# A graph layer on one core: rows of every 68th quad fetched by SyncE, another order on VectorE, another start

## The chip, the core and the metric

The kernel runs on one core of a Trainium2 chip. The metric is the device time of one execution in microseconds, the median of several. The engines are named as in the profile: PE (TensorE, matmuls; PEld is its weight load), DVE (VectorE), ACT (ScalarE), POOL (GpSimd) and SP (SyncE, which only issues DMAs here). [...]

## What is computed

One message-passing layer on a graph of 12,500 nodes and 400,000 edges, the edges sorted by destination. Each node has 160 features: 64 scalars and 32 vectors of three. Everything is float32.

```python
h_s = s @ lin1_ws * a * _inv(S_IN)                      # per node, and h_v likewise
hid = jax.nn.silu(edge_scalars @ fc_w1 * _inv(R))       # per edge
w = hid @ fc_w2 * _inv(FC_HID)                          # 224 weights per edge
es = h_s[edge_src]; ev = h_v[edge_src]                  # rows of the source nodes
m_s1 = w1 * es * e0                                     # messages, five kinds
...
agg_s = jax.ops.segment_sum(mid_s, edge_dst, num_segments=n) * inv_nn
o_s = agg_s @ lin2_ws * a * _inv(S_MID)                 # per node, and o_v likewise
...
x = _layernorm(x + gated)
```

The host only lays inputs out (transposes, tiles of 128 edges, each edge on one of the 128 partitions).

## The kernel before

**The start.** Node features come transposed in six chunks of 2048 nodes and one of 212 (`CH`, `starts`): `xa` (scalars and two of the three vector components) in two halves of columns, and `xz` (the third component) in four quarters on four groups of 32 partitions. PE multiplies them with the block-diagonal weights `l1` and `l1z` (L316, L331), DVE scales the result with the node attribute into `ht` (L319, L334), and a DMA on ACT's queue stores `ht` to the table `h_tab` in DRAM (L345). SP's queue holds, in this order: `rows`, the first destination of each block of three tiles (three strided loads of single elements, L254, L255); the features; the first indices `idx`, edge attributes `eat` and edge scalars `es`; the weights of the edge MLP, `w1` and `w2`, in twelve loads. `dt`, all destinations, is loaded on ACT's queue after the stores (L351). From it DVE makes `rel`, the place of each edge's destination relative to its block's base (L387). All engines' instructions of the start stand in the order in which they are written (`manual_schedule`).

**The loop.** 3125 tiles of 128 edges are taken in 782 steps of up to four tiles, a *quad*: two tiles of each half of a chunk of 24 tiles. A step `n` does, in this order:

- `fetch(n + 4)`: loads of a chunk's `es` (two DMAs of 384 KB) and of the next 72 tiles' `idx` and `eat` when a quad four steps ahead is the first to need them.
- `gather` (L427): four indirect DMAs on POOL, each fetching the 128 rows of one tile from `h_tab` (640 bytes each) into `hg`, in a pool of four buffers (`deep`). POOL does nothing else in the loop.
- `weights` (L440): PE multiplies the hidden layer `hid` with `w2` into `pw` (two buffers in PSUM).
- `products` (L450, L458): DVE multiplies `pw` with `hg` into `pr`, four instructions.
- `select_quad`: DVE compares `rel` with a ramp into a one-hot matrix `oh` (L504) and multiplies it with the edge attributes into `sel` (L507).
- up to two additions of finished blocks to the sums `acc` (L546), which read their place from registers.
- `sum_up` for the quad of two steps before (L514): PE multiplies `sel` with `pr` into `pa`, the segment sum of a block; ACT copies a finished pair of blocks to `sa` (L706).
- `hide(n + 2)` (L418, L420): the hidden layer of a later pair of quads, on PE and ACT.
- turning blocks over (`pt` L523, copies `tt` L526, L528), and for 16 blocks at a time the second linear map (`po` L538, copy `os` L541), for whose bases DVE loads registers from `rows` (L730).
- some steps also carry the self connection and the end of finished nodes (transposes, gates, layer norm, store).

On PE, DVE, ACT and POOL the order of the loop is the written one; on SP the framework orders the loads. A DMA of SP or ACT takes one of eight semaphores in turn, and waits until the DMA that had it before has landed.

A path for edges whose destinations lie too far apart follows the loop; with these inputs it isn't entered.

Of the kernel before, what the change touches and what calls it, by code (L numbers as in the profile page):

```python
# [10 lines left out]
F32 = mybir.dt.float32  # L11
I32 = mybir.dt.int32
I16 = mybir.dt.int16
BF16 = mybir.dt.bfloat16
AF = mybir.ActivationFunctionType
OP = mybir.AluOpType
AX = mybir.AxisListType
# [17 lines left out]
CT = 2 * SIDE  # L35
AHEAD = 3 * CT
NF = 4

MARGIN = 128
NO = 16  # L40
# [13 lines left out]
def gnn_kernel(  # L54
# [40 lines left out]
    in_order = ctx.enter_context(ExitStack())  # L95
    in_order.enter_context(tc.manual_schedule(
        engines={ENG.PE, ENG.DVE, ENG.Activation, ENG.Pool, ENG.SP}))
    at = consts.tile([P, NT], F32, name="at")
    nc.scalar.dma_start(at, attr)

    l1 = consts.tile([P, P], F32, name="l1")
    nc.vector.memset(l1, 0.0)
    nc.scalar.dma_start(l1[:S, :S], lin1_ws)
    for i in range(2):
        r = slice(S + i * V, S + (i + 1) * V)
        nc.scalar.dma_start(l1[r, r], lin1_wv)
    scales = [(l1[:S], 1.0 / math.sqrt(S)), (l1[S:], 1.0 / math.sqrt(V))]

    def scale():
        for m, by in scales:  # L110
            nc.vector.tensor_scalar_mul(m, m, by)
        scales.clear()

    def block_diagonal(name, w, n, scale, queue=nc.scalar):
        k = w.shape[0]
        m = consts.tile([n * k, n * k], F32, name=name)
        nc.vector.memset(m, 0.0)
        for i in range(n):
            queue.dma_start(m[i * k:(i + 1) * k, i * k:(i + 1) * k], w)
        if scale != 1.0:  # L120
            scales.append((m, scale))
        return m

    l1z = block_diagonal("l1z", lin1_wv, 4, 1.0 / math.sqrt(V))
    for m, by in scales:
        nc.scalar.mul(m, m, by)
    scales.clear()


    rel = consts.tile([P, TT], I16, name="rel")  # L130
    rows = consts.tile([1, NB], I32, name="rows")
    early = consts.tile([1, 1], F32, name="early")
# [84 lines left out]

    ess = {}

    def load_chunk(c):  # L220
        if c in ess:
            return
        t0, halves = chunks[c]
        es = ess[c] = loads.tile([2 * S, SIDE * P], F32, name="es")
        for half, n in enumerate(halves):
            to = es[half * S:(half + 1) * S]
            e0 = (t0 + half * halves[0]) * P
            nc.sync.dma_start(to[:, :n * P], es_t[:, e0:e0 + n * P])


    ident = consts.tile([P, P], F32, name="ident")
# [16 lines left out]
                   base=0, channel_multiplier=0)  # L248
    nc.gpsimd.iota(share[:, even:], pattern=[[RATE, NB - even]], base=even * RATE, channel_multiplier=0)

    with nc.allow_non_contiguous_dma(reason="the first destination of each block"):
        firsts = dst[0:1, 0:(even - 1) * BT + 1:BT].rearrange("o (c h k) -> o h c k", k=KB, h=2)
        for half in range(2):
            nc.sync.dma_start(in_pairs(rows[:, :even])[:, half], firsts[:, half])  # L254
        nc.sync.dma_start(rows[:, even:], dst[0:1, even * BT:(NB - 1) * BT + 1:BT])  # L255


    U = 4
    dt = ends_pool.tile([P, TT], I32, name="dt")
    lo = ends_pool.tile([P, NB], F32, name="lo")  # L260
# [2 lines left out]
    with tc.tile_pool(name="nodes", bufs=len(starts)) as nodes, tc.tile_pool(  # L263
        name="nodes_ps", bufs=6, space=PSUM
    ) as nps, tc.tile_pool(name="z_ps", bufs=2, space=PSUM) as zps:
        loaded = []
        for c0 in starts:
            cn = min(CH, N - c0)
            quarters = 4 if cn == CH else 1
            assert quarters == 4 or cn <= U * P  # L270
            xa = nodes.tile([P, CH], F32, name="xa")
            for b0 in range(0, cn, CH // 2):
                b1 = min(b0 + CH // 2, cn)
                nc.sync.dma_start(xa[:S, b0:b1], xs_t[:, c0 + b0:c0 + b1])
                nc.sync.dma_start(xa[S:, b0:b1], xv_t[:2 * V, c0 + b0:c0 + b1])
            xz = nodes.tile([P, U * P], F32, name="xz")
            cq = cn // quarters
            for q in range(quarters):
                nc.sync.dma_start(xz[q * V:(q + 1) * V, :cq],
                                  xv_t[2 * V:, c0 + q * cq:c0 + (q + 1) * cq])  # L280
            loaded.append((c0, cn, quarters, cq, xa, xz))
        index(0)
        load_chunk(0)
        for half in range(2):
            r = slice(half * S, (half + 1) * S)
            nc.sync.dma_start(w1[r, r], fc_w1)
            at_c = 0
            for a, b in ((64, 128), (0, 64), (192, 224), (160, 192), (128, 160)):
                nc.sync.dma_start(w2[r, half, at_c:at_c + b - a], fc_w2[:, a:b])
                at_c += b - a  # L290

        def bases():

            base_f = ends_pool.tile([1, NB], F32, name="base_f")
            nc.vector.tensor_copy(base_f, rows)
            for b0 in range(0, NB, U * P):
                b1 = min(NB, b0 + U * P)
                ps = nps.tile([P, U, P], F32, name="hp").rearrange("p u c -> p (u c)")
                nc.tensor.matmul(ps[:, :b1 - b0], ones, base_f[:, b0:b1], start=True, stop=True)
                nc.scalar.copy(lo[:, b0:b1], ps[:, :b1 - b0])  # L300
            nc.vector.tensor_sub(share, rows, share)
            nc.vector.tensor_reduce(early, share, AX.X, OP.min)
            nc.vector.tensor_scalar(early, early, -float(MARGIN), None, op0=OP.is_lt)

        for c0, cn, quarters, cq, xa, xz in loaded:
# [19 lines left out]
                                            at[:n, first + full:first + full + 1], None, op0=OP.mult)  # L325

            pz = zps.tile([P, U, 4, V], F32, name="pz")
            k = quarters * V
            for u in range(-(-cq // P)):
                n = min(P, cq - u * P)  # L330
                nc.tensor.matmul(pz[:n, u, :quarters].rearrange("p q c -> p (q c)"),  # L331
                                 xz[:k, u * P:u * P + n], l1z[:k, :k], start=True, stop=True)
            if quarters == 4:
                nc.vector.tensor_mul(  # L334
                    ht[:, :, P:].rearrange("p (q u) c -> p u q c", q=4), pz,
# [5 lines left out]
            if cn > full * P:  # L341
                n = cn - full * P
                nc.vector.tensor_scalar(ht[:n, full, P:], pz[:n, full, 0],
                                        at[:n, first + full:first + full + 1], None, op0=OP.mult)
            nc.scalar.dma_start(  # L345
                h_tab[c0:c0 + full * P, :].rearrange("(q p) d -> p q d", p=P), ht[:, :full])
            if cn > full * P:
                nc.scalar.dma_start(h_tab[c0 + full * P:c0 + cn, :], ht[:n, full])


    nc.scalar.dma_start(dt, dst)  # L351
    iota = consts.tile([P, W], F32, name="iota")
    nc.vector.tensor_copy(iota, iota_i)
    nc.vector.tensor_scalar_mul(w2, w2, 1.0 / math.sqrt(64))

    scs = consts.tile([S, V3], F32, name="scs")
    nc.sync.dma_start(scs, sc_ws)
# [65 lines left out]
    def gather(pool, idx):  # L423
# [5 lines left out]
                in_offset=bass.IndirectOffsetOnAxis(ap=i, axis=0))  # L429
        return hg  # L430

    def weights(psum, hid, slots):

        pw = psum.tile([P, Q, 256], F32, name="pw")
        n = len(slots)
        for t in range(0, n, 2):
            half, c = slots[t]
            m = min(2, n - t)
            assert half == 0 and all(slots[t + k] == (k, c) for k in range(m))
            nc.tensor.matmul(pw[:, t:t + m, :NWT], hid[:m * S, c * P:(c + 1) * P], w2[:m * S, :m],  # L440
                             start=True, stop=True)
        return pw
# [52 lines left out]
            sorted_eat[a0] = eas  # L495
        return sorted_eat[a0]

    def select_quad(pool, tiles):

        n = len(tiles)  # L500
        t0 = slot_of[tiles[0][0]]
        u = t0 % AHEAD
        oh = pool.tile([P, Q, W], F32, name="oh4")[:, :n]
        nc.vector.tensor_tensor(oh, rel[:, t0:t0 + n, None].to_broadcast([P, n, W]),  # L504
                                iota[:, None, :].to_broadcast([P, n, W]), op=OP.is_equal)
        sel = pool.tile([P, Q, 4, W], F32, name="sel", bufs=3)
        nc.vector.tensor_mul(  # L507
            sel[:, :n], oh[:, :, None, :].to_broadcast([P, n, 4, W]),
            by_slot(tiles[0][0])[:, u:u + n, :, None].to_broadcast([P, n, 4, W]))
        return sel  # L510
# [112 lines left out]
    with tc.tile_pool(  # L623
        name="fin", bufs=1
    ) as fin, tc.tile_pool(
        name="late", bufs=2
    ) as late, tc.tile_pool(name="edge", bufs=2) as edge, tc.tile_pool(
        name="deep", bufs=4
# [26 lines left out]
        def fetch(n):  # L655

            if n < len(steps):
# [2 lines left out]
                    load_chunk(c)  # L660
                for t, _, _ in tiles:
                    ahead(t)

        def hide(n):

# [109 lines left out]
                    turning.extend(job[:nt])  # L775
                    doing.extend(job[nt:])

        with tc.manual_schedule(engines={ENG.PE, ENG.DVE, ENG.Activation, ENG.Pool}):
            fetch(0)
            hide(0)  # L780
            waits = []
            pieces = list(range(0, N, CHN))
            products_due = []
            checks = farthest(late)
            for n, (c, i, tiles) in enumerate(steps):
                if 2 <= n < 2 + ZP // 2:
                    for k in range(2):
# [1 line left out]
                if n in checks:  # L789
                    checks[n]()  # L790
                fetch(n + 4)
                hg = gather(deep, [index(t) for t, _, _ in tiles])
                pw = weights(pw_ps, hids[c, i // 2], [(half, u - i // 2 * 4) for _, half, u in tiles])

                rest = turning.pop(0)() if turning else None
# [3 lines left out]
                def first(n=n):  # L799
                    if rest:  # L800
                        rest()
                    ready.extend(add_up(n))

                pr = products(edge, pw, hg, len(tiles), [first, lambda n=n: ready.extend(add_up(n))])
                sel = select_quad(edge, tiles)
                for a in ready:
                    add(*a)
                if step_on:
                    step_on()
                begin()  # L810
# [153 lines left out]
```

## Time and profile before

| | |
|---|---|
| median of 15 runs | 5032.44 us (5026.09 to 5071.89) |
| the profiled execution | 5034.64 us, span 5032.8 us |
| granted TensorE clock, mean | 0.883 |
| PE, DVE, POOL, ACT busy | 79%, 48%, 60%, 18% of the span |
| gathers (L427) | 3125, 967 ns mean, first at 78 us |
| first products (L450) | 92 us |
| DMA, 20 to 80 us | 95% busy, 259 GB/s |
| DMA, 100 to 4990 us | 31% busy, 80 GB/s |

Times are from the start of the span. A line of the waits has: the engine and line that waited, what ended the wait, us in total, times, longest. "issue" means that the engine waited for nothing that the profile shows, "remote" that a semaphore's update could not be put down to an instruction. A line of the timeline has: start, length, engine, line, operation, output and inputs, how many instructions are merged, and in brackets the engine's idle time before and what ended it. [...]

### The profile page before, as it was taken

To read this page: it belongs to the slowest core of one execution; us is meant where nothing else is said; L and a number is where in the kernel's file an instruction comes from. 1 tells how busy PE (TensorE), PEld (TensorE's weight loads), DVE (VectorE), ACT (ScalarE), POOL (GpSimd) and SP (SyncE) were. 2 spreads that over 40 slices of the span, in tenths; PEclk is the share of its full clock that TensorE was granted. 3 is DMA by queue.
4 is the path that set the end of the run, shared out by engine and by line. 5 is a ranking of instruction groups with operands and counts; after the bars stand their busy time and mean duration, and the time that the engine had idled before them with its cause. 6 is when DMAs were issued, how large, how long until landed. Compare 5 with 4: busy or idle time off the path is not lost. (4 is left out here: it accounts for less than half of the span.)

```text
span 5032.8 us, 47627 instructions
## 1 busy us (share of the span) xinstructions
PE 3978.8 (79%) x14291; PEld 1698.3 (34%) x14291; DVE 2433.0 (48%) x6374; ACT 926.7 (18%) x2463; POOL 3026.4 (60%) x3134
## 2 busy tenths in 40 slices
PE   5788787887778877887777877878878787878877
PEld 3333333333333333333333333333333333333333
DVE  4544444544544544544544544444544544544544
ACT  1211111211211111212111111111121211211212
POOL 3666665666666666665665665666666666666663
PEclk7898898988988888989898888989988898889888
DMA  7233332332333333333333233323333332333221
GB/s 196 76 81 77 78 83 74 83 85 75 81 80 81 81 81 78 83 79 79 81 81 80 75 85 77 77 78 86 78 82 80 80 86 75 81 81 80 76 72 51
DMA packets 241211, 411.77 MB, mean 82 GB/s; under 512 B 74200, under 2 KB 171876, under 8 KB 240820
## 3 DMA queue, kind: packets, MB, share of 16 engines
q0 software_dynamic: 150000, 256.20, 19.5%
q1 hardware_dynamic: 77666, 142.75, 11.7%
q10 hardware_dynamic: 13282, 9.69, 0.7%
q8 instruction: 119, 1.95, 0.2%
q14 instruction: 144, 1.18, 0.1%
HBM read 392.40 MB, written 16.00 MB: 81 GB/s over the span
## 5 line engine op out<-in xcount | busy, mean ns | idle before, releaser
L427 POOL DMA_INDIRECT hg<-h_tab,idx x3125 | 3021.7, 967 | 1962.5 <-DVE oh L504 984.3
L440 PE MATMUL pw<-w,hid 128*128 128x448 f32 x3126 | 1519.0, 613 | 294.9 <-ACT hid L420 98.5
L450 DVE TENSOR_TENSOR pr<-pw,hg 128x512 f32<-128x512 f32 x782 | 539.4, 690 | 2332.5 <-remote 1093.3
L514 PE MATMUL pa<-pr,sel 128*64 128x416 f32 x6250 | 1384.7, 557 | 101.1 <-issue 65.7
L458 DVE TENSOR_TENSOR pr<-pw,hg 128x384 f32<-128x384 f32 x2346 | 1154.3, 547 | 2.3 <-issue 2.2
L440 PEld LDWEIGHTS pw<-w,hid 128*128 128x128 f32 x3126 | 608.1, 213 | 837.3 <-issue 659.1
L514 PEld LDWEIGHTS pa<-pr,sel 128*64 128x64 f32 x6250 | 406.8, 144 | 1011.8 <-issue 869.5
L523 PE MATMUL pt<-ident,sa 128*128 128x128 f32 x2084 | 357.9, 297 | 296.8 <-ACT hid L420 162.5
L706 ACT COPY sa<-pa 128x416 f32<-128x416 f32 x521 | 265.9, 510 | 1751.3 <-remote 657.9
L418 PE MATMUL ph<-es,w 128*128 128x512 f32 (+1 forms) x784 | 453.2, 661 | 71.0 <-ACT tt L528 38.1
L523 PEld LDWEIGHTS pt<-ident,sa 128*128 128x128 f32 x2084 | 255.4, 149 | 634.9 <-issue 339.2
L420 ACT ACTIVATE hid<-ph 128x512 f32<-128x512 f32 x392 | 234.5, 598 | 1079.2 <-remote 612.6
L538 PE MATMUL po<-tt,l 128*96 128x256 f32 (+5 forms) x1496 | 369.4, 397 | 43.8 <-ACT tt L528 30.5
L507 DVE TENSOR_TENSOR sel<-oh,eas 128x256 f32<-128x256 f32 x782 | 338.5, 433 | 42.7
L526 ACT COPY tt<-pt 128x192 f32<-128x192 f32 x521 | 166.2, 319 | 770.9 <-remote 231.5
L538 PEld LDWEIGHTS po<-tt,l 128*96 128x96 f32 (+1 forms) x1496 | 239.4, 172 | 191.9 <-issue 84.9
L418 PEld LDWEIGHTS ph<-es,w 128*128 128x128 f32 x784 | 120.0, 193 | 340.2 <-issue 255.0
L546 DVE TENSOR_TENSOR acc<-acc,os 96x32 f32 x1042 | 195.0, 187 | 26.1 <-ACT os L541 6.9
L504 DVE TENSOR_TENSOR oh<-rel,iota 128x64 f32<-128x64 int16 x782 | 170.1, 217 | 0.5 <-issue 0.5
L572 PE MATMUL pp<-ident,acc 96*128 96x96 f32 x196 | 38.6, 285 | 107.7 <-DVE acc L546 48.8
L528 ACT COPY tt<-pt 128x64 f32<-128x64 f32 x521 | 117.0, 225 | 0.0
L541 ACT COPY os<-po 96x512 f32<-96x512 f32 (+2 forms) x68 | 38.3, 564 | 394.0 <-PE po L538 83.5
(77 smaller groups left out, 648.9 us busy)
## 6 DMA issues: line engine op xcount, KB each, us to landing
es<-in_es_t_dram SPq DMA_DIRECT2D x260, 384.0 KB
hg<-h_tab,idx POOLq DMA_INDIRECT x3125
h_tab<-ht ACTq DMA_DIRECT2D x6, 1280.0 KB
xt<-in_x_dram SPq DMA_DIRECT2D x23, 320.0 KB
out_dram<-y SPq DMA_DIRECT2D x23, 320.0 KB
xv<-in_xv_t_dram SPq DMA_DIRECT2D x25, 187.5 KB
xs<-in_xs_t_dram SPq DMA_DIRECT2D x25, 125.0 KB
xa<-in_xs_t_dram SPq DMA_DIRECT2D x12, 256.0 KB
```

What stands on the lines that cost most here:

```text
L418: nc.tensor.matmul(ph[:k, c], w1[:k, :k], es[:k, t0 * P + c0 * P:t0 * P + c1 * P], start=True, stop=True)
L420: nc.scalar.activation(hid[:k, c], ph[:k, c], AF.Silu, scale=1.0 / math.sqrt(64))
L427: nc.gpsimd.indirect_dma_start(out=hg[:, t, :], out_offset=None, in_=h_tab, in_offset=bass.IndirectOffsetOnAxis(ap=i, axis=0))
L440: nc.tensor.matmul(pw[:, t:t + m, :NWT], hid[:m * S, c * P:(c + 1) * P], w2[:m * S, :m], start=True, stop=True)
L450: nc.vector.tensor_mul(two, pw[:, :n, :2 * S].rearrange("p t (k c) -> p t k c", k=2), hg[:, :n, None, :S].to_broadcast([P, n, 2, S]))
L458: nc.vector.tensor_mul(pr[:, :n, first:first + V3].rearrange("p t (i c) -> p t i c", i=3), pw[:, :n, None, 2 * S + k * V:2 * S + (k + 1) * ...
L507: nc.vector.tensor_mul(sel[:, :n], oh[:, :, None, :].to_broadcast([P, n, 4, W]), by_slot(tiles[0][0])[:, u:u + n, :, None].to_broadcast([P ...
L514: nc.tensor.matmul(pa[half * ROWS:(half + 1) * ROWS, :NPR], sel[:, t].rearrange("p k w -> p (k w)"), pr, start=start, stop=stop)
L523: nc.tensor.transpose(pt[:, four * P:four * P + k], sa[:k, c:c + P], ident[:k, :k])
L538: nc.tensor.matmul(po[:, k, :nb], l2[r, terms[to, part, four]], a[:, :nb], start=(n == 0), stop=(n == len(of) - 1))
L546: nc.vector.tensor_add(window, window, os[:, :, b])
L706: nc.scalar.copy(sa, pas.pop(j)[:, :NPR])
```

## The change

It has three parts.

1. **Rows by SP.** The quads 76, 144, ..., 756 (eleven) no longer gather on POOL. Eight steps before the first of these fetches SP loads the four tiles' indices as rows of one partition each (`places`), DVE multiplies them by the 640 bytes of a row, and SP, 66 steps before the quad, begins to fetch its 512 rows one by one into `hq` (one buffer): every second step it loads 16 indices into registers and issues 16 DMAs of one row, with the address from the register. The loop's order on SP is now the written one too.
2. **DVE's order.** A step does its products, then `sel`, then the additions, then the one-hot matrix of the next step. The additions are two in even steps and one in odd ones.
3. **The start.** The first chunk's features are the first loads on SP; the loads of a chunk are one for each of `xs_t` and `xv_t` and one for `xz` (whose 128 partitions now hold the quarters interleaved, as `l1z` does). The strided loads of `rows` are gone: row 0 of `dt` is loaded on ACT's queue and DVE picks `rows` from it. `w2` is loaded as a whole (`raw`) and scaled into place by ten DVE instructions. The stores of `h` (but the last, of 84 rows, which goes to SP), the first chunk's `es` and `dt` are issued by POOL, in front of the gathers.

```diff
+OWN = 68
+BATCH = 16
+EVERY = 2
...
-    with nc.allow_non_contiguous_dma(reason="the first destination of each block"):
-        firsts = dst[0:1, 0:(even - 1) * BT + 1:BT].rearrange("o (c h k) -> o h c k", k=KB, h=2)
-        for half in range(2):
-            nc.sync.dma_start(in_pairs(rows[:, :even])[:, half], firsts[:, half])
-        nc.sync.dma_start(rows[:, even:], dst[0:1, even * BT:(NB - 1) * BT + 1:BT])
...
-            for b0 in range(0, cn, CH // 2):
-                b1 = min(b0 + CH // 2, cn)
-                nc.sync.dma_start(xa[:S, b0:b1], xs_t[:, c0 + b0:c0 + b1])
-                nc.sync.dma_start(xa[S:, b0:b1], xv_t[:2 * V, c0 + b0:c0 + b1])
+            nc.sync.dma_start(xa[:S, :cn], xs_t[:, c0:c0 + cn])
+            nc.sync.dma_start(xa[S:, :cn], xv_t[:2 * V, c0:c0 + cn])
...
+        load(starts[0])
+        at = consts.tile([P, NT], F32, name="at")
+        nc.scalar.dma_start(at, attr)
...
+        nc.scalar.dma_start(dt[0:1], dst[0:1])
+        for c0 in starts[1:]:
+            load(c0)
         index(0)
-        load_chunk(0)
+        raw = ends_pool.tile([2 * S, NWT], F32, name="raw")
         for half in range(2):
             r = slice(half * S, (half + 1) * S)
             nc.sync.dma_start(w1[r, r], fc_w1)
-            at_c = 0
-            for a, b in ((64, 128), (0, 64), (192, 224), (160, 192), (128, 160)):
-                nc.sync.dma_start(w2[r, half, at_c:at_c + b - a], fc_w2[:, a:b])
-                at_c += b - a
+            nc.sync.dma_start(raw[r], fc_w2)
...
-            nc.scalar.dma_start(
+            nc.gpsimd.dma_start(
                 h_tab[c0:c0 + full * P, :].rearrange("(q p) d -> p q d", p=P), ht[:, :full])
             if cn > full * P:
-                nc.scalar.dma_start(h_tab[c0 + full * P:c0 + cn, :], ht[:n, full])
-
-
-    nc.scalar.dma_start(dt, dst)
+                nc.sync.dma_start(h_tab[c0 + full * P:c0 + cn, :], ht[:n, full])
+
+
+    load_chunk(0, nc.gpsimd)
+    nc.gpsimd.dma_start(dt, dst)
...
+    def places(pool, n):
+        at_bytes = pool.tile([Q, P], I32, name="at_bytes")
+        for k, (t, _, _) in enumerate(steps[n][2]):
+            g, u = divmod(t, GT)
+            with nc.allow_non_contiguous_dma(reason="the indices of one tile"):
+                nc.sync.dma_start(at_bytes[k:k + 1], src[g][:, u:u + 1].rearrange("p u -> u p"))
+        return at_bytes
+
+    def rows_of(pool, at_bytes):
+        hq = pool.tile([P, Q, D], F32, name="hq", bufs=1)
+        flat_hq = hq.rearrange("p t d -> p (t d)").bitcast(U8)
+
+        def job(t, p0):
+            _, values = nc.values_load_multi_w_load_instructions(
+                at_bytes[t:t + 1, p0:p0 + BATCH], engines=[ENG.SP], min_val=0,
+                max_val=(N - 1) * row_bytes,
+                skip_runtime_bounds_check_because="every entry of src is the index of a node")
+            for p, v in enumerate(values, p0):
+                nc.sync.dma_start(flat_hq[p:p + 1, t * row_bytes:(t + 1) * row_bytes],
+                                  by_bytes[ds(v, row_bytes)][None])
+
+        return hq, [lambda t=t, p0=p0: job(t, p0) for t in range(Q) for p0 in range(0, P, BATCH)]
...
+        def fetch_rows(n):
+            for m in own:
+                if n == max(1, m - OWN - 6):
+                    at_of[m] = places(mine, m)
+                if n == m - OWN + 2:
+                    nc.vector.tensor_scalar_mul(at_of[m], at_of[m], float(row_bytes))
+                    hq_of[m], jobs = rows_of(mine, at_of[m])
+                    rows_due.extend((m, job) for job in jobs)
+            if n % EVERY == 0 and rows_due:
+                rows_due.pop(0)[1]()
...
-        with tc.manual_schedule(engines={ENG.PE, ENG.DVE, ENG.Activation, ENG.Pool}):
+        with tc.manual_schedule(engines={ENG.PE, ENG.DVE, ENG.Activation, ENG.Pool, ENG.SP}):
...
-                hg = gather(deep, [index(t) for t, _, _ in tiles])
+                fetch_rows(n)
+                hg = hq_of.pop(n) if n in own else gather(deep, [index(t) for t, _, _ in tiles])
...
-                    ready.extend(add_up(n))
-
-                pr = products(edge, pw, hg, len(tiles), [first, lambda n=n: ready.extend(add_up(n))])
-                sel = select_quad(edge, tiles)
+                    for _ in range(2 - n % 2):
+                        ready.extend(add_up(n))
+
+                pr = products(edge, pw, hg, len(tiles), [first, lambda: None])
+                sel = select_quad(edge, tiles, oh)
                 for a in ready:
                     add(*a)
+                if n + 1 < len(steps):
+                    oh = one_hot(edge, steps[n + 1][2])
```

## The prediction, made before the changed kernel ran

> **What bounds the kernel now.** I read the page's busy shares first, then the waits, then the timeline of a stretch in the middle, then that of the start.
>
> ```profile
> PE 3978.8 (79%) x14291; PEld 1698.3 (34%) x14291; DVE 2433.0 (48%) x6374; ACT 926.7 (18%) x2463; POOL 3026.4 (60%) x3134
> ```
> ```profile
> DVE pr L450 <- remote: 1093.3, 127, 14.3
> POOL hg L427 <- DVE oh L504: 984.3, 241, 10.7
> POOL hg L427 <- issue: 932.6, 2797, 72.8
> ...
> DVE pr L450 <- DMA hg<-h_tab,idx: 123.9, 63, 6.9
> ```
>
> No engine is full by the shares. But POOL's 60% leaves out 0.30 us of "issue" after every gather: in the timeline gathers follow each other every 1.25 us, so a quad's four take 5.0 us. From the first (78 us) to the last (4989 us) POOL does only two things: 3022 + 860 us of gathering (the 72.8 us before the first gather taken off), and 984 us in 241 pauses (4.1 us each) in which all four `hg` buffers are full. A quad takes 4911 / 782 = 6.28 us. DVE waits directly for a gather in only 124 us; its long waits (remote, PE) are for PE's signal. The timeline shows what these are:
>
> ```profile
> 1023.62 5.25 PE L538 MATMUL po<-tt,l 128*96 128x256 f32 x22
> ...
> 1031.36 0.95 POOL L427 DMA_INDIRECT hg<-h_tab,idx  x1 [0.30 <-issue]
> ...
> 1034.55 0.58 ACT L541 COPY os<-po 96x512 f32<-96x512 f32 x1 [10.13 <-PE pw L440]
> 1034.61 0.69 DVE L450 TENSOR_TENSOR pr<-pw,hg 128x512 f32<-128x512 f32 x1 [11.05 <-PE pw L440]
> ...
> 1036.97 0.95 POOL L427 DMA_INDIRECT hg<-h_tab,idx  x1 [4.66 <-DVE oh L504]
> ```
>
> PE's last `po` matmul ends at 1028.87, yet ACT may read `po` only at 1034.55 and DVE the next `pw` at 1034.61: 5.7 us with the work done and its signal not there. POOL's last gather had ended at 1032.31. The same happens at 1013.84 (last gather ended at 1012.51). Then DVE takes its 2.2 us of products, a buffer is free, POOL goes on. So PE and DVE stand still, POOL fills what buffers there are, and the signal comes about when POOL is quiet. Counting POOL's unbroken runs of gathers in its timeline: 102 of 248 are of exactly 16, the four quads that `deep` has buffers for; they hold 408 of the 782 quads, 52%.
>
> **Rows of every 68th quad by SP.** Quads 76, 144, ... 756, eleven, lose their gathers: 44 x 1.25 = 55 us of POOL's work. What it is worth lies between two ends. If the loop goes at POOL's cycle (16 gathers, a pause), an own quad rides along free: 6.28 us x 11 = 69 us. If PE sets the pace, nothing. I take 52% of the 69, the share of quads in full 16-gather runs: **-36 us**. Below nothing it could go by the next paragraph.
>
> SP pays: 11 x 512 row DMAs and 352 loads of 16 register values. SP's DMAs take 0.348 us (idx, median) to 0.582 us (es); DVE's register load of block bases (L730) 1.1 us. A job of 16 rows is so 16 x 0.348 + 1.1 = 6.7 to 16 x 0.582 + 1.1 = 10.4 us, and has two steps, 12.6 us. SP mostly waits today. Each row DMA also waits for the eighth DMA before it, which binds only from 8 x 0.35 = 2.8 us of landing time on. The loop's loads are now in SP's hand-written order behind jobs and output stores: the `es` of a chunk is asked for four steps and needed two steps before its first quad, a cover of 12.6 us; an index column is needed when a buffer frees, and then POOL loses what SP is late. I cost this at nothing while a job fits. The waits added: SP's first load of a batch waits for DVE's scaling of the indices (eleven small DVE operations, nearest row 0.20 us for 32x96, 2 us in all, in DVE's idle half) and for `hq` to be free; behind it stand `es` loads, asked for with that cover; DVE's products of an own quad wait for 512 rows whose last job is issued four steps before.
>
> The row says POOL's issue time is the scarce thing and DMA engines are not (31% busy from 100 to 4990 us). [...]
>
> **DVE's order.** `oh` moves behind `sel` and the additions of the step before: 0.22 us x 782 is neither added nor removed; it now falls into DVE's wait for `pw`, where there is one. Nobody waits for `sel` at once, since a quad's `pa` matmuls come two steps later: PE's `pa` waits that DVE's oh and sel end are 32.5 us (37 times) and 22.0 us (25 times). At most 62 x 0.22 = 14 us; I take **-5**. POOL's release hangs on the products, which stay first. The additions (2 or 1 a step instead of up to 2) keep their total.
>
> **The start.**
>
> ```profile
> 7.22 0.53 SPq L274 DMA_DIRECT2D xa<-in_xs_t_dram  x1
> ...
> 34.01 3.75 PE L316 MATMUL hp<-l,xa 128*128 128x128 f32 x16 [8.22 <-DMA xa<-in_xv_t_dram]
> ...
> 78.13 1.13 POOL L427 DMA_INDIRECT hg<-h_tab,idx  x1 [72.77 <-issue]
> ...
> 85.49 6.24 DVE L387 TENSOR_TENSOR rel<-dt,lo 128x260 int16<-128x260 int32 x12
> ...
> 92.13 0.67 DVE L450 TENSOR_TENSOR pr<-pw,hg 128x512 f32<-128x512 f32 x1
> ```
>
> The first features are issued at 7.2 us, behind strided one-row loads; from 20 to 80 us DMA is 95% busy at 259 GB/s, PE waiting for features. So the start is transfer-bound: features first saves 7.2 - 0.8 = 6.4 us. Fewer, larger loads and one load instead of five for the MLP weights change no bytes. DVE's extra copies (three rows, nearest row 0.68 us for 1x1042; ten scalings for one of 0.39) lie in its waits of 8 to 14 us. The stores of `h` move from ACT (0.37 us each to issue) to POOL, in front of the first `es`, of `dt` and of all gathers. No row shows a plain store from POOL. A gather of 128 rows takes it 0.95 us; a store names 2048 rows of the same 640 bytes. If cost goes by instruction, six stores are 7.5 us; if by rows, 15.2 us each. A chunk's load and store are 2.6 MB, 10.1 us at 259 GB/s, so up to that the stores hide. Beyond it the first gather comes at about 13 + 6 x 15.2 = 104 plus 2 to 3 us instead of 78: +28. I take the hidden case, **-6** (from -8 to +28); `dt` lands later relative to the stores but, with them, earlier than 85.5, and `rel` (6.2 us) follows it as now.
>
> [...]
>
> **Sum.** The profiled execution took 5034.64 us (span 5032.8); the median of 15 runs, 5032.44, is 2.2 lower. 5034.6 - 36 - 5 - 6 - 2.2 = **4985 us**.
>
> **Rivals.**
> - A, the rows are hidden anyway: PE (3979 us busy, 79%, at a granted clock of 0.883) sets the pace and POOL only pauses longer, its 984 us growing by 55. For it: only 124 us of direct waits for gathers. Against it: 52% of quads in full-buffer runs. 5034.6 - 11 - 2.2 = 5021.
> - B, SP becomes the bound: 68 steps are 427 us; less some 17 us for `es`, `idx`, `eat` and stores, a job may take 12.8 us (0.73 us a row). Each microsecond beyond costs 11 x 32 = 352 us: 13.5 us gives 5034.6 + 246 - 13 = 5268, slower. For it: no row shows a DMA with a register address. Against: both ends of the job lie below.
> - C, the quiet moments go: if PE's signals also wait for SP's rows, which are under way in over half of the time, every pause grows; 0.2 us more in each of 241 eats the gain, 1 us gives 5034.6 + 241 - 47 - 2 = 5226. Against: from 8 to 66 us SP issues loads every 0.5 to 2 us with DMA 95% busy, and DVE follows PE within 0.2 to 1.0 us there.
> - D, POOL's stores cost by rows: 4985 + 34 = 5019.
>
> **Numbers.** Forecast 0.52, A 0.20, B 0.08, C 0.12, D 0.08. 0.3% (15 us) is what a measurement of this kernel can tell from no change. The forecast's own range goes from 5032.4 - 69 - 14 - 8 = 4941 to A's side; with A and D, 0.80 lie between 4940 and 5060 (the +28 with nothing else gained). Faster: most of the forecast and a little of A, 0.53; same: A, D and the forecast's edge, 0.26; slower: B, C and the worst of D, 0.21.
>
> **What would show it.** Right: gathers down to 3081, POOL's busy down by some 43 us and its pauses hardly longer; row DMAs on SP at 0.35 to 0.6 us, a job well under 12.6 us; DVE's products of own quads without a wait for `hq`; first gather near 72 us, first product near 86. Wrong: pauses longer by what the gathers lost (A), SP solid between batches and POOL waiting for `idx` or PE for `es` (B), longer waits on remote (C), h stores of 15 us on POOL (D).

## The result, and the profile after

The changed kernel takes **5195.58 us** (median of 12 runs) against 5040.5 us (62 runs): ratio **1.0306**, 95% interval 1.0286 to 1.0326. It is slower by 155 us, where 47 us of gain were predicted; the range (4940 to 5060 us) doesn't hold it. The profiled execution has a span of 5212.0 us at a granted clock of 0.868.

One thing must be known to read what follows. The sets of runs fell on several chips and times. In three of them the kernel before takes 4081 to 4091 us, and in the traces PE's signals come at once (0.03 us after its matmuls on average in after_again); in the others, those of the prediction among them, it takes 5032 to 5130 us (medians) and PE's signals come late (2.0 us on average in before). I call these *prompt* and *late* signals, and compare times only within a set; where ratios or traces of two sets stand side by side, the text says so or names both runs.

The page's line of busy time:

```profile
PE 3966.2 (76%) x14291; PEld 1713.0 (33%) x14291; DVE 2351.3 (45%) x6397; ACT 922.3 (18%) x2463; POOL 2972.1 (57%) x3100
```

POOL has lost its 44 gathers, and every engine's share has fallen: all wait more. For what, the waits tell (us in total, times, longest):

```profile
DVE pr L494 <- remote: 1356.2, 163, 17.6
POOL hg L442 <- DVE pr L502: 1188.1, 278, 11.0
POOL hg L442 <- issue: 885.2, 2765, 6.9
...
POOL hg L442 <- DMA hq<-h_tab: 25.1, 7, 8.9
PE ph L433 <- DMA es<-in_es_t_dram: 19.5, 3, 16.0
POOL hg L442 <- DMA idx<-in_src_dram: 15.2, 3, 6.4
```

POOL's pauses on full buffers (ended by DVE's `oh` in the trace of before, by its products in that of after, as DVE's order changed) grew from 241 of 4.08 us to 278 of 4.27 us, +204 us. From its first to its last gather POOL took 4911 us before and 5102 after. The 191 us between are these 204, less 64 of gathering, and 51 of more issue time and of smaller waits. The waits for something that SP fetched late (the last three lines) are 60 us, 16 of them a single wait for the first `es`, which start_2, without rows, has too (14.0 us). So the loop isn't simply waiting for SP's loads.

A late signal like the one shown of before, in the timeline of after:

```profile
595.82 25.91 SPq L471 DMA_DIRECT2D hq<-h_tab  x32
...
599.37 1.62 PE L563 MATMUL pa<-pr,sel 128*64 128x416 f32 x8
...
601.88 1.67 PE L484 MATMUL pw<-w,hid 128*128 128x448 f32 x4
...
605.02 0.66 PE L572 MATMUL pt<-ident,sa 128*128 128x128 f32 x4
...
612.47 0.95 POOL L442 DMA_INDIRECT hg<-h_tab,idx  x1 [0.30 <-issue]
615.39 0.51 ACT L772 COPY sa<-pa 128x416 f32<-128x416 f32 x1 [16.58 <-remote]
...
616.14 0.69 DVE L494 TENSOR_TENSOR pr<-pw,hg 128x512 f32<-128x512 f32 x1 [10.61 <-remote]
...
618.49 0.95 POOL L442 DMA_INDIRECT hg<-h_tab,idx  x1 [5.07 <-DVE pr L502]
```

PE's last matmul ends at 605.7; the last of the twelve `pa` matmuls whose sum ACT copies has ended at 601.0, and the `pw` that DVE's products wait for at 603.5. Yet PE, DVE and ACT stand still until 615.4, two microseconds after POOL's last gather ended (613.4). All this time SP works through two jobs of rows that take 25.9 us.

From the semaphore events of the trace one can take, for each PE instruction that signals, the time from its modelled end to PE's next event: 2.0 us on average before, 2.7 us after (100 to 5000 us). Within after it is 3.0 us where the matmul ends during a job of rows (1777 signals) and 1.8 us where it ends between jobs (660). These averages are too high, and more so after: the traces lack some events (2236 of PE's are there for 2597 signals before, 2165 for 2592 after), and where one is missing the next is taken for it. The instructions that wait give a measure without events, the time from PE's modelled end, or from the waiting engine's own last work if that is later, to their start. ACT's copies of `pa` are late by 1.71 us before and 1.77 after (0.09 in after_again, a run with prompt signals below). DVE's products, less what they wait for gathers, are late by 1.90 and 2.12 us, but by 2.14 in no_rows_3 too, a run below without rows. So the lateness is there; that the rows make the average signal later can't be told from this.

SP's rows, in the answer for their lines (min/median/max ns, first and last start), after:

```profile
L471 SPq MOVE hq<-h_tab x5632: 2/29/1412, 142.5 to 5007.0; - x195
L471 SPq DMA_DIRECT2D hq<-h_tab x5632: 2/227/1398, 142.6 to 5007.8; - x195
```
```profile
L466 SPq TENSOR_LOAD <-at_bytes x352: 3/1216/1896, 141.3 to 4992.8; - x176
```

The medians make a job of 16 x 0.256 + 1.2 = 5.3 us. But the longest instructions, and the starts, tell another thing: from the first to the last DMA of a job it takes 9.4 us (median), as SP itself is held up every few rows. Its waits in the queue's view sum to 4087 us before and 685 us after: SP went from mostly idle to 87% taken.

The start did better than predicted:

```profile
0.75 0.59 SPq L239 DMA_DIRECT2D xa<-in_xs_t_dram  x1
...
62.20 1.04 POOL L442 DMA_INDIRECT hg<-h_tab,idx  x1 [6.92 <-issue]
...
69.46 6.34 DVE L402 TENSOR_TENSOR rel<-dt,lo 128x260 int16<-128x260 int32 x12 [12.61 <-ACT eas L530]
...
80.67 0.68 DVE L494 TENSOR_TENSOR pr<-pw,hg 128x512 f32<-128x512 f32 x1
```

The first gather is 15.9 us earlier, the first product 11.5 us. POOL's stores of `h` (L354) took 1.15 us each in the median and 1.39 at most, not 15.

### The profile page after: what moved, and what is told of

The parts are those of the page before. It is cut to its first block, busy times and chain, and to the rows that moved or that the text cites. A ratio compares the mean times of both kernels' runs of the same rounds, so it can differ in the third digit from the quotient of the medians.

```text
span 5212.0 us, 59292 instructions
## 1 busy us (share of the span) xinstructions
PE 3966.2 (76%) x14291; PEld 1713.0 (33%) x14291; DVE 2351.3 (45%) x6397; ACT 922.3 (18%) x2463; POOL 2972.1 (57%) x3100
## 5 line engine op out<-in xcount | busy, mean ns | idle before, releaser
L442 POOL DMA_INDIRECT hg<-h_tab,idx x3081 | 2957.9, 960 | 2150.6 <-DVE pr L502 1188.1
L563 PE MATMUL pa<-pr,sel 128*64 128x416 f32 x6250 | 1353.5, 551 | 93.2 <-issue 47.3
L502 DVE TENSOR_TENSOR pr<-pw,hg 128x384 f32<-128x384 f32 x2313 | 1137.1, 547 | 0.0
L572 PE MATMUL pt<-ident,sa 128*128 128x128 f32 x2084 | 374.1, 308 | 534.5 <-ACT hid L435 298.3
L572 PEld LDWEIGHTS pt<-ident,sa 128*128 128x128 f32 x2084 | 267.3, 156 | 876.7 <-ACT hid L435 345.6
L587 PE MATMUL po<-tt,l 128*96 128x256 f32 (+5 forms) x1496 | 394.0, 416 | 91.1 <-ACT tt L577 88.0
L587 PEld LDWEIGHTS po<-tt,l 128*96 128x96 f32 (+1 forms) x1496 | 251.3, 180 | 254.6 <-ACT tt L577 105.3
L556 DVE TENSOR_TENSOR sel<-oh,eas 128x256 f32<-128x256 f32 x782 | 325.9, 417 | 0.0
L595 DVE TENSOR_TENSOR acc<-acc,os 96x32 f32 x1042 | 206.6, 198 | 20.0 <-ACT os L590 7.1
L753 DVE TENSOR_TENSOR acc<-acc,psc 96x500 f32<-96x500 f32 x50 | 33.5, 670 | 180.4 <-remote 81.8
L590 ACT COPY os<-po 96x512 f32<-96x512 f32 (+2 forms) x68 | 38.3, 564 | 398.2 <-PE po L587 200.1
```

The source lines that it names most:

```text
L442: nc.gpsimd.indirect_dma_start(out=hg[:, t, :], out_offset=None, in_=h_tab, in_offset=bass.IndirectOffsetOnAxis(ap=i, axis=0))
L502: nc.vector.tensor_mul(pr[:, :n, first:first + V3].rearrange("p t (i c) -> p t i c", i=3), pw[:, :n, None, 2 * S + k * V:2 * S + (k + 1) * ...
L556: nc.vector.tensor_mul(sel[:, :n], oh[:, :, None, :].to_broadcast([P, n, 4, W]), by_slot(tiles[0][0])[:, u:u + n, :, None].to_broadcast([P ...
L563: nc.tensor.matmul(pa[half * ROWS:(half + 1) * ROWS, :NPR], sel[:, t].rearrange("p k w -> p (k w)"), pr, start=start, stop=stop)
L572: nc.tensor.transpose(pt[:, four * P:four * P + k], sa[:k, c:c + P], ident[:k, :k])
L587: nc.tensor.matmul(po[:, k, :nb], l2[r, terms[to, part, four]], a[:, :nb], start=(n == 0), stop=(n == len(of) - 1))
```

## The experiments

The theories: **T1**, SP's rows cause the loss, by lengthening PE's late signals (rival C); **T2**, DVE's new order does it; **T3**, SP's written order makes loads late.

### Parts of the change, with prompt signals

Edits to the kernel after: no rows; DVE's old order; SP's order left to the framework.

```diff
-    own = [n for n in range(OWN + 8, len(steps) - 4, OWN) if len(steps[n][2]) == Q]
+    own = []                                            # a_start, b_no_rows, d_start_order
...
-                sel = select_quad(edge, tiles, oh)      # a_start, c_old_order (additions too)
+                sel = select_quad(edge, tiles, one_hot(edge, tiles))
...
-        with tc.manual_schedule(engines={..., ENG.Pool, ENG.SP}):
+        with tc.manual_schedule(engines={..., ENG.Pool}):      # a_start, d_start_order
```

The start alone:

> Only the new start; the loop is that of the kernel before (no rows by SyncE, one-hots and additions in the old order, SyncE's loads of the loop in the scheduler's order). The first gather came 15.9 us earlier in the kernel after (62.2 against 78.1 us), the first product 11.5 us. All theories: 11 to 16 us faster than before, 5024 to 5029 us. If the loop lost its time to something that the start leaves behind (buffers placed elsewhere, h_tab written by another queue), this run loses 100 us or more as well.

Start, DVE's order, SP's order:

> The kernel after without rows by SyncE: all quads are gathered by GpSimd; new start, new order on VectorE, SyncE's loop loads in written order. T1 (SyncE's rows make PE's late signals later and more): the whole 190 us of the loop come back, 5020 to 5030 us, pauses of POOL as before (241 of 4.1 us). T2 (VectorE's order): it stays near 5190 us, pauses 270 or more. T3 (SyncE's written order makes es or idx late): it stays near 5190 us too, with PE waiting for es or POOL for idx.

Start, rows, SP's order:

> The kernel after with VectorE's old order: one-hot directly ahead of its selection, up to two additions in each step between the products. Rows by SyncE and the new start stay. T1 (rows): still 5180 to 5200 us. T2 (VectorE's order): back to 4960 to 5030 us, since the rows then bring what they save or nothing. T3 (SyncE's order): still 5180 to 5200 us.

Start and DVE's order:

> New start and VectorE's new order alone: no rows, SyncE's loop loads in the scheduler's order as before. T1 (rows) and T3 (SyncE's order): 5015 to 5030 us, as the start alone within 0.3%. T2 (VectorE's order): near 5190 us.

| with before at 4082.25 us | us | ratio (95%) |
|---|---|---|
| a_start | 4060.20 | 0.9949 (0.9932 to 0.9965) |
| d_start_order | 4049.18 | 0.9924 (0.9908 to 0.9941) |
| b_no_rows | 4047.15 | 0.9919 (0.9902 to 0.9935) |
| c_old_order | 4006.16 | 0.9819 (0.9802 to 0.9835) |

Before takes 19% less time here than in the prediction's runs, and no part of the change costs anything. The expectations were written for late signals, so these runs can't part the theories. The start is worth 22 us, DVE's order 11 (d against a), SP's order nothing that can be told (2), the rows 54 (c against a). The kernel after itself, in a set of its own:

> The kernel after, unchanged, because the first four runs fell on a chip where the kernel before takes 4082 us instead of 5040 us, with PE's signals prompt (99% within 0.03 us of the modelled end). On such a chip, additive parts give 4082 - 21 (start) - 12 (order) - 56 (rows, c_old_order against the start) = about 3993 us, ratio 0.978. If the order on VectorE harms the rows it ends above c_old_order's 4006 us. On a chip as in the prediction (before 5040 us) it repeats the ratio 1.03.

The same kernel with no rows, on the same chip:

> The kernel after without rows by SyncE, again, beside the kernel after on the same chip. On a chip with late signals (before 5040 us): T1 (rows lengthen the late signals) 5020 to 5030 us, ratio 0.995 to 1.0; T2 and T3 (order on VectorE, SyncE's order) 5190 us, ratio 1.03. On a chip with prompt signals: ratio 0.992 as before.

The rows fetched and not read:

```diff
-                hg = hq_of.pop(n) if n in own else gather(deep, [index(t) for t, _, _ in tiles])
+                hg = gather(deep, [index(t) for t, _, _ in tiles])
```

> SyncE fetches the rows as in the kernel after, but they are not read: GpSimd gathers every quad. This is the price of the rows without their saving. On a chip with late signals: T1 makes it at least as slow as the kernel after, ratio 1.03 to 1.05; T2 and T3 likewise 1.03, as without rows. On a chip with prompt signals the rows cost nothing: ratio 0.992 as the version without rows, within 0.3%; if the row DMAs get in the way of gathers there too, more.

No gathers in the loop:

```diff
+            still = gather(late1, [index(t) for t, _, _ in steps[0][2]])
...
-                hg = hq_of.pop(n) if n in own else gather(deep, [index(t) for t, _, _ in tiles])
+                hg = still
```

> Leaves out all gathers but those of the first quad, whose rows serve every quad (wrong features of the edges, all other work the same), and the rows by SyncE. If PE's late signals come from GpSimd's gathers, they are prompt here on any chip, and the time is set by PE: its 3670 us busy plus start and end, 3750 to 3850 us on both kinds of chip. If they come from something else (clock, DMA loads), then on a chip with late signals it stays above 4500 us.

| with before at 4081.24 us | us | ratio (95%) |
|---|---|---|
| after_again | 3994.99 | 0.9786 (0.9770 to 0.9802) |
| no_rows_2 | 4046.44 | 0.9913 (0.9897 to 0.9930) |
| rows_unused | 4044.52 | 0.9906 (0.9889 to 0.9922) |
| no_gathers | 3611.05 | 0.8847 (0.8833 to 0.8862) |

With prompt signals the change takes 2.1% off (2.0 to 2.3), and the rows cost nothing: fetched for nothing they leave the time as it is without them, used they take off 51 us. no_gathers ended below the 3750 to 3850 us expected: PE is busy for 3545 us in it, not 3670. The page's line of busy time and two of the waits of after_again:

```profile
PE 3663.5 (92%) x14291; PEld 1588.4 (40%) x14291; DVE 2346.0 (59%) x6397; ACT 940.4 (24%) x2463; POOL 2971.0 (74%) x3100
```
```profile
POOL hg L442 <- issue: 843.4, 2767, 0.3
...
DVE pr L494 <- DMA hg<-h_tab,idx: 611.6, 250, 8.1
```

POOL gathers without a pause from 62 to 3958 us and DVE waits for gathers: a plain GpSimd-bound loop, at 1.25 us a gather. PE's events come 0.03 us after its matmuls on average, and the same 16 rows take SP 4.9 us instead of 9.4. The busy times of DVE, ACT and POOL are within 2% of those of the slower trace; PE's is 303 us shorter, at a granted clock of 0.967 in place of 0.868, and the rest of the difference is waiting. And the events themselves: after left 77,164 semaphore events here and 26,210 there, for one and the same program.

### Rows in other doses, with late signals

> The kernel after with rows for every 51st quad (15 quads instead of 11), a job of 16 rows in two of three steps. On a chip with prompt signals GpSimd's gathers set the pace and each quad taken off saves 4 x 1.25 = 5.0 us less what it was paused anyway: 3995 - 4 x 4.7 = 3976 us, ratio 0.974, SyncE still at 170 us of 257. On a chip with late signals: T1 (rows) slower than the kernel after, ratio 1.04; T2 and T3 (order on VectorE, SyncE's order): ratio 1.03 or a little less, as the kernel after.

```diff
-OWN = 68
+OWN = 51
...
-            if n % EVERY == 0 and rows_due:
+            if n % 3 and rows_due:
```

> The kernel after with rows for every 136th quad (5 quads), a job every fourth step. On a chip with prompt signals 3995 + 6 x 4.7 = 4023 us, ratio 0.986. On a chip with late signals: T1 about half of the loss, ratio 1.01 to 1.02; T2 and T3 ratio 1.03.

```diff
-OWN = 68
+OWN = 136
...
-EVERY = 2
+EVERY = 4
```

> Each job fetches 16 consecutive rows of the table with one DMA in place of 16 DMAs of a row (wrong rows; same bytes, same register loads). On a chip with prompt signals as the kernel after, 3995 us within 0.3%, since a row DMA is hidden there. On a chip with late signals: T1 by the number of DMAs 4990 to 5010 us, ratio 0.99 to 0.995; if it is the register loads, the order on VectorE or SyncE's order, it stays at ratio 1.03.

```diff
-            for p, v in enumerate(values, p0):
-                nc.sync.dma_start(flat_hq[p:p + 1, t * row_bytes:(t + 1) * row_bytes],
-                                  by_bytes[ds(v, row_bytes)][None])
+            nc.sync.dma_start(hq[p0:p0 + BATCH, t], h_tab[p0:p0 + BATCH])
```

The rows alone, put into the kernel before (with `places`, `rows_of`, `fetch_rows` and SP in the written order, as in the change):

> The kernel before with the rows by SyncE alone (and SyncE's loads in written order, which the rows need): old start, old order on VectorE. On a chip with prompt signals 4081 - 51 = 4030 us, ratio 0.987. On a chip with late signals: T1 ratio 1.03 to 1.035; T2 (VectorE's order) 0.99 to 1.0; T3 (SyncE's order) 1.03.

| with before at 5129.57 us | us | ratio (95%) |
|---|---|---|
| rows_51 | 6005.94 | 1.1697 (1.1664 to 1.1730) |
| rows_only | 5313.12 | 1.0336 (1.0300 to 1.0373) |
| rows_136 | 5187.85 | 1.0096 (1.0067 to 1.0124) |
| one_dma | 5139.14 | 1.0024 (0.9997 to 1.0052) |

Here the signals were late again, and the rows are the culprit, as T1 says: the rows alone lose what the whole change loses, fewer rows at half the pace lose less, and the same bytes in a sixteenth of the DMAs lose next to nothing, although its eleven quads need no gathers either. So T2 and T3 are not needed. T1's sizes held less well: one_dma was expected at 0.99 to 0.995, and rows_136 lies just under its 1.01 to 1.02. In rows_only a good part of the loss is POOL waiting for `idx` behind the rows (`idx` and rows take SP's eight semaphores in turn, 778 DMAs on each in the trace of after, so the trace names either; POOL reads no `hq`): 71.7 and 38.3 us, against 25.1 and 15.2 in after.

```profile
POOL hg L431 <- DMA hq<-h_tab: 71.7, 9, 13.5
```

rows_51 lost four times what T1 said, in another way. Its waits:

```profile
POOL hg L442 <- DVE pr L502: 1584.9, 281, 25.7
...
PE ph L433 <- DMA es<-in_es_t_dram: 826.0, 95, 24.4
...
POOL hg L442 <- DMA hq<-h_tab: 445.3, 35, 20.3
```

PE waits 826 us for `es`, 19.5 in after. A job takes 9.35 + 1.2 us (means) and comes every one and a half steps, which at 6.3 us are 9.4: SP can't keep up, and the loads behind the rows are late. SP waits in all 407 us of 6003. That is rival B, one notch of pace beyond the change.

> The kernel after without rows by SyncE (new start, new order on VectorE, SyncE's loads in written order), for a chip with late signals, where rows alone measured 1.034 and one DMA in place of sixteen 1.002. T1 in full (the rows are the whole loss): 0.990 to 0.996 of before. T2 (VectorE's order costs too on such a chip): above 1.003. On a chip with prompt signals: 0.991 again.

Rows at fixed addresses, without register loads:

```diff
-            _, values = nc.values_load_multi_w_load_instructions(...)
-            for p, v in enumerate(values, p0):
-                nc.sync.dma_start(flat_hq[p:p + 1, t * row_bytes:(t + 1) * row_bytes],
-                                  by_bytes[ds(v, row_bytes)][None])
+            for p in range(p0, p0 + BATCH):
+                nc.sync.dma_start(hq[p:p + 1, t], h_tab[9 * p:9 * p + 1])
```

> The kernel after with 16 one-row DMAs in each job at fixed addresses (wrong rows), and no loads into SyncE's registers. On a chip with late signals: if the number of DMAs is what counts, ratio 1.025 to 1.035 as the kernel after; if the register loads or register addresses count, 0.995 to 1.005. On a chip with prompt signals: 0.978 as the kernel after.

Before took 5110.12 us; no_rows_3 5115.37 us, ratio 1.0003 (0.9978 to 1.0028); const_rows 5177.82 us, 1.0155 (1.0115 to 1.0196). Neither expectation was met. Without rows the kernel is neither faster nor slower, so the rows are the whole loss of 3%. DMAs of one row make about half of it by their number (1.0155, against 1.0306 and 1.0336 in other sets). The other half goes with register loads and addresses together (one_dma, which has the loads and few DMAs, loses 0.2%, at most 0.5% by its interval, with its gathers saved); they keep SP's jobs longer, 9.4 us from the first to the last DMA in the kernel after against 6.8 in const_rows. Both are held up far beyond 16 x 0.256 us.

How the rows' cost travels isn't settled. POOL's pauses, in no_rows_3 and in one_dma (two sets), are longer in sum where gathers are fewer:

```profile
POOL hg L442 <- DVE pr L502: 1115.6, 260, 11.0
```
```profile
POOL hg L442 <- DVE pr L500: 1183.0, 266, 10.8
```

From the first product to the last it takes 4912 us before and 5099 after. DVE's products, less what they wait for gathers, are late by 1486 us in sum before and 1661 after, and DVE waits 723 and 909 us for PE to end its work on `pw` in the first place. In one set, const_rows against no_rows_3, it is 1741 against 1670 us late, and 839 against 820 waiting for PE. So late signals take part, but 1670 of these microseconds are there without any rows, and that the rows make each signal later, as T1 says, is not shown. Nor do jobs against the time between them prove it: jobs start in every second step, and before, without rows, the products of even steps are late by 1.43 us and those of odd steps by 2.68 (waits for gathers included).

### Where the late signals come from

> Leaves out all gathers but those of the first quad, and the rows by SyncE, as on the chip with prompt signals, where it took 3611 us. On a chip with late signals: if GpSimd's gathers make PE's signals late, they are prompt here too and the time is within 1% of 3611 us, ratio 0.70 to 0.72 of a before of 5110 us; if PE is slower there for another reason (its clock), it takes 4300 us or more and PE's signals stay late.

> Only the new start, for a chip with late signals, where start, VectorE's order and SyncE's order together measured 1.000 instead of the 0.992 of a chip with prompt signals. If the start's 21 us are gained there too, ratio 0.996; then the orders cost what is gained. If the start gains nothing there, 1.000.

Before took 5044.16 us. start_2: 5034.95 us, ratio 0.9985 (0.9955 to 1.0015); the start's 22 us can't be seen there, nor excluded in full. no_gathers_2: 3609.97 us, ratio 0.7163 (0.7119 to 0.7207), on the microsecond what it took with prompt signals. Its page and first wait:

```profile
PE 3543.4 (98%) x14291; PEld 1568.2 (43%) x14291; DVE 2341.0 (65%) x6386; ACT 939.3 (26%) x2463; POOL 18.1 (1%) x23
```
```profile
DVE pr L494 <- PE pw L484: 1155.2, 769, 6.6
```

PE's signals come 0.02 us after its matmuls, and PE sets the pace. So the lateness needs GpSimd's gathers, and without them neither PE nor DVE nor the chip is slow. Which part of a gather does it (POOL's instruction, the moving of rows, its events) wasn't tried apart, nor were SP's rows without gathers.

Last, in the version without rows, whether the number of `hg` buffers sets the loss:

```diff
-        name="deep", bufs=4
+        name="deep", bufs=6                             # deep3: 3
...
-        oh = pool.tile([P, Q, W], F32, name="oh4")[:, :n]
+        oh = pool.tile([P, Q, W], F32, name="oh4", bufs=1)[:, :n]
```

> The version without rows (new start, new order) with six buffers of gathered quads in place of four; the one-hot keeps one buffer in place of two, to make room. On a chip with late signals: if GpSimd runs until all buffers are full and the signals then come in a pause of a fixed 4 to 5 us, a cycle is 6 x 5.0 + 5 = 35 us for six quads, 5.8 us a quad in place of 6.3, and the time 4700 to 4800 us, ratio 0.92 to 0.94. If the pause grows with the cycle (the work that was held up has to be made good), 5110 us, ratio 1.00. On a chip with prompt signals: 0.991, as with four.

> The same with three buffers. On a chip with late signals: by the fixed pause a cycle is 3 x 5.0 + 5 = 20 us, 6.7 us a quad, 5350 to 5450 us, ratio 1.05 to 1.07; if the pause goes with the cycle, ratio 1.00 to 1.01. On a chip with prompt signals: 0.99 to 1.00, since products follow a gather within a quad or two there.

Signals were prompt in this set (before 4091.33 us): deep6 4045.66 us, ratio 0.9888 (0.9872 to 0.9905), deep3 4057.54 us, 0.9911 (0.9895 to 0.9928). That is no_rows_2 again, as expected for prompt signals; the question that they were made for, late signals, stays open.

**What stays open.** Why signals are late in some sets: the chip numbered 3 had them prompt in one set and late in another, so it isn't the chip by its number alone. Every run here was recorded by the profiler, and the trace of after holds 26,210 semaphore events where that of after_again holds 77,164, for one and the same program. Whether the recording takes part in the lateness no run shows: none was made without the profiler, and so the cause isn't settled.

**Which version.** With prompt signals the kernel after is the fastest of those that do all the work (0.9786). With late signals none beat the kernel before beyond its interval (start_2, 0.9985). The change without rows gains 0.8 to 0.9% in the one case and loses nothing that can be told in the other.

## Why the prediction was wrong, step by step

- **What bounds the kernel**: read rightly for the trace at hand. POOL fills its buffers while a signal is awaited, and without gathers the signal comes at once (0.02 us, no_gathers_2). But I took the late signal for a trait of the kernel; with prompt signals the same kernel has none and takes some 950 us less.
- **Rows, -36: the step that failed.** Two halves of it. The saving depends on the signals: with prompt ones it was 51 us of the 55 that 44 gathers last, more than the 36 that I took; with late ones next to nothing, net of the register loads, as one_dma (no gathers for eleven quads, few DMAs) and no_rows_3 differ by 0.2%, within their intervals. There the pauses grew by about what the gathers lost (rival A): 1115.6 us in no_rows_3, 1183.0 in one_dma (two sets), +67. And the price, set at nothing "while a job fits": a job did fit (9.4 + 1.2 us, just past my 10.4, against 12.6), the waits for SP's loads were 60 us, and still the rows cost 3.0% (1.0306 against 1.0003). So "a job fits" wasn't the condition under which rows are free: that was prompt signals (rows_unused 0.9906, no_rows_2 0.9913). What the cost goes by is the number of one-row DMAs (const_rows, 1.0155 of 1.0306) and, for the other half, register loads and addresses; by which waits it reaches the loop stays open.
- **Rival C** comes nearest and was given 0.12. It priced 0.2 us more a pause as eating the gain; the pauses became 0.2 us longer *and* 37 more. But no_rows_3, in a slower set, has 260 pauses of 4.29 us without any rows, so their length alone doesn't show C's mechanism. I dismissed it with the start of the kernel, where SP's loads are dense and DVE follows PE within 0.2 to 1.0 us. But no gathers run there, and the lateness needs gathers (0.02 us without them, no_gathers_2): the row of the trace that I used lacked the one thing that matters. Within the loop the trace of before had no stretch with dense SP traffic, so C's cost was unknown and deserved more chance and a wider range.
- **DVE's order, -5**: 11 us with prompt signals, within its bound of 14. With late signals it can't be told from zero (0.9985 and 1.0003, each +-0.003).
- **The start, -6**: first gather 15.9 us earlier and 22 us of gain with prompt signals; mis-sized. I counted only the first load's delay and not the fewer and earlier loads behind it; that these make the difference wasn't tried apart. With late signals 0.15%, uncertain.
- **Rival B** isn't the main part of what slowed the change (60 us of waits for SP's loads, 16 of them at the start), but rows_51 shows it one step away. **Rival D** fell: 1.15 us a store, and the +28 us of the start's range didn't come.
- **The gain with prompt signals**, 86 us, isn't the forecast of 47 come true: POOL gathers without a pause there, a condition that the prediction did not weigh.
- **Small transfers.** With prompt signals the small rows cost nothing (rows_unused 0.9906, no_rows_2 0.9913), with late ones one DMA for sixteen takes the loss from 3.1% to 0.2% (two sets). SP's own waits for row DMAs to land were 67.4 us in all (116 waits, after).

## What to carry to other kernels

Before adding many small DMAs to a loop, ask not only whether the issuing engine has time: look also for a waiting engine whose producer ended long ago. Here DVE stood still for 5.7 us after PE's last matmul (before); signals, not work, were the scarce thing, and the price of more DMAs, put at nothing, was unknown until it was measured: 3.0%. A stretch that is to excuse a risk must contain all that the risk needs (here gathers *and* SP's loads). Repeat the kernel before with every comparison: the sign of this change depends on a condition that the code doesn't show (ratio 0.9786 with prompt signals, 1.0306 with late ones).

## What the runs showed of the hardware

- A gather left 16 semaphore events (49,652 on GpSimd's DMA semaphores for 3125 gathers), a one-row DMA of SP 2 (20,544 with 5632 rows, 8824 without), both with prompt signals. The trace of before, which lacks events, agrees: between a gather's issue and the next one on its semaphore there are never more than 16, and 84 times 16. A quad of rows so costs some 1065 events where four gathers cost 64. Whether these events hold SP up when signals are late, which would stretch its jobs, wasn't tried.
- In these runs, which all do the same 14,291 matmuls, the mean granted clock is the higher the larger PE's busy share: 0.992 at 98% (no_gathers_2), 0.967 at 92% (after_again), 0.883 at 79% (before), 0.868 at 76% (after), 0.827 at 68% (rows_51).
- Waiting on PE, ACT starts its copies of `pa` 0.09 us late on average with prompt signals (after_again) and 1.71 us late with late ones (before). DVE's signals to POOL show no such delay: in before, all 233 pauses of more than 1 us between gathers end 0.27 us after the last product of the quad whose buffer they need.
